# Fewer and larger loads of queries and keys in a two-layer attention kernel on Trainium2

## The chip, the cores and the metric

One core of a Trainium2 chip runs the whole program. The metric is device time in microseconds (us) of one execution. The core has five engines with a queue of instructions each: PE (matrix products), DVE (vector operations), ACT (activations), POOL (further elementwise work) and SP, which in this kernel does nothing but issue DMA transfers. An engine takes its instructions strictly in order. The DMA transfers themselves run on 16 DMA engines, here called lanes.

## The reference

A sequence `x` of 2048 rows of width 256 goes through two transformer layers with 16 heads of width 16. Cut to what matters:

```
layer 0, h = first or second half of the rows (1024 each):
  x_h += gate * attend(q(norm(x_h)), k(norm(x_h)), v(norm(x_h))) @ wo      # stage 0: own half
  x_h += gate * attend(q(norm(x_h)), k(norm(x_other)), v(norm(x_other)))   # stage 1: other half
  x_h += gate * mlp(norm(x_h))
layer 1, all 2048 rows:
  scores = where(mask == 0, -1e9, q @ k.T / 4)
  x = norm(x + softmax(scores) @ v @ wo)                                   # stage 2: masked
  x = norm(x + attend(q(x), k(ctx), v(ctx)) @ wo)                          # stage 3: 1601 context rows
  x = norm(x + mlp(x))
```

`attend` is a softmax over the keys. For it the kernel finds the maximum of every row of scores first, and computes the scores a second time, transposed, less that maximum.

## The kernel before

**Units.** The rows are cut into 4 blocks of 512 (`BLK`), the 16 heads into 4 groups `g` of 4 heads. A unit is one block and one group in one of the four stages; the first block of the masked stage is done in two parts, each over half the keys, which gives 68 units. Keys lie in two slots of 1024 (`SLOT`). A unit of stage 0 or 1 sees one slot, one of stages 2 and 3 both. `stream` (line 1411) walks the units. A unit has two steps for each 128 keys (16 steps for 1024 keys). In each step PE computes one tile of transposed scores of this unit, ACT takes its exponential, PE multiplies an earlier tile by the values, and PE and DVE make one or more tiles of the row maxima of the next unit (`take_maxima`). The maxima of a unit begin four steps before the unit ahead of it does (`AHEAD`), that is in step 12 of a 16-step unit for the unit after next.

**Order.** The order on every engine is written by hand. `after(step)` (1472) runs once a step: it runs what stands in the list `later` and is due, sends at most one transfer from the list `transfers` (`load_ready`, line 989), and advances one of the background generators, which do projections, norms, the MLPs and the next stage's queries, keys and values. What has no place of its own on SP is issued in the order in which the program comes to it. SP waits at the head of its queue for the data and the buffer of its next transfer, with all others behind it.

**Through DRAM.** `halves` (461) computes queries and keys for a block, splits each into a high and a low part (`hi`, `lo`, in buffers tagged `half`, three of them) and stores them to `q_dr` and `k_dr`. `load_queries` (1002) loads a unit's queries, each high and each low part into two places, with 8 transfers of 16 partitions, 64 KB each; it is called in step 1 of a unit for the unit after next, into one of three buffers `q`. `load_slot` (932) puts 8 transfers of keys (16 partitions, 128 KB each) and two or more of values for one group and one slot into `transfers`. Four such sets of keys come ready in a row when the last block behind a slot is done.

**Sums.** In step 2 of the next unit `copy_sums` (1285) lets ACT copy a unit's accumulated products to `sums` (a `half` buffer). Four transfers bring the softmax sums to `weights`, four more the products to `oT`. Five steps later DVE inverts `weights` (`invert`, 1327), `rd` goes to DRAM (`rd_dr`) and comes back spread over 64 partitions (`rd_rows`, line 1337, whose source has an outermost dimension of 4), eight steps later POOL multiplies (`divide`, 1340). After ten or eleven steps the block's projection may start. In the unit done in parts, `as_rows` (1177) also sends the maxima on with 12 small transfers (`mh`, line 1194) and adds them on DVE four steps later.

**Masks.** `mask_rows` (1025) loads a 128x512 piece of the mask into one of two buffers `raw`, and POOL turns it into a bias. `mask_part` (1049) puts eight of these one step apart; `pair` in `maxima` (1123) does the next block's 16 pieces in group 3, two at a time where the unit is a part.

Of the kernel before, what the change touches and what calls it, by code (L numbers as in the profile page):

```python
# [12 lines left out]
F32 = mybir.dt.float32  # L13
# [9 lines left out]
P = 128  # L23
# [54 lines left out]
def two_layers(ctx: ExitStack, tc: tile.TileContext, a: dict, out: bass.AP):  # L78
# [76 lines left out]

    made = sb.tile([P, P], F32, tag="half", bufs=3, name="made")
    make_identity(nc, made)
# [43 lines left out]
    def half(shape, dtype=F32, name="half"):  # L201
        return sb.tile(shape, dtype, tag="half", bufs=3, name=name)

# [24 lines left out]
    def load_attn(n, raw_tile, between=None):  # L228
        w = a[f"w_attn{n}"]
        t = sb.tile([P, 2, 2, 2, P], F32, tag="w_qk", name="w_qk")  # L230
        for k in range(2):
            raw = raw_tile()
            nc.sync.dma_start(raw, w[:, k * 2 * BLK : (k + 1) * 2 * BLK])
            src = raw.rearrange("p (w g c i r) -> p w c g i r", w=2, g=NG, c=2, i=2)


            def copies(k=k, src=src):
                for qk in range(2):
                    for c in range(2):
                        nc.gpsimd.tensor_copy(  # L240
                            t[:, k, qk, c, :].rearrange("p (g i d) -> p g i d", g=NG, i=2),
                            src[:, qk, c, :, :, :HD],
                        )

            if between is None:
                copies()
            else:
                first_copies.append(copies)
# [75 lines left out]
    for g in range(NG):  # L324
        for i in range(2):
            at = (2 * g + i) * HD
            for c in range(2):
                (nc.sync, nc.scalar)[i].dma_start(qkb[at : at + HD, :, :, c], src[g, i, c, :HD])
    m = one_ps()
# [418 lines left out]
    def chain_cross(b):  # L748
# [4 lines left out]
        if last:  # L753
# [4 lines left out]
        yield from normalize(xn, t, 1e-6)  # L758
        hT = yield from transposed(xn, mod=(2, b // 2))
        yield from mlp(  # L760
            mlp0[0], 0, AF.Gelu_apprx_tanh, hT, gated(rows["m0"], t, b),

            (lambda: mask_part(1)) if last else None,
        )
# [28 lines left out]
    def chain_context(n):  # L793

        if n == 0:

            yield 20
            load_attn(3, attn_raw)
        r0, r = CTX[n]
        c = stage([P, TPB, D], name="c")  # L800
# [4 lines left out]
        if r % P:  # L805
            nc.sync.dma_start(c[: r % P, full, :], a["ctx"][r0 + full * P : r0 + r, :])
        yield 3
        hT = yield from transposed(c, n=r)
# [123 lines left out]
    def load_slot(kind, st, g, slot):  # L932
# [7 lines left out]
        def keys(c, i):  # L940
            at = 64 * c + HD * i
            nc.sync.dma_start(
                kT[g][slot][at : at + HD, :, :even].bitcast(F32),
                d[c, i % 2, 2 * g * HD : (2 * g + 2) * HD, :even].rearrange(
                    "(q d) t -> d q t", d=HD
                ),
            )
# [23 lines left out]
        if kind == "keys":  # L971
            if st == 2 and slot == 1 and g in (1, 2):
                kT[g][slot] = sb.tile([P, 2, SLOT], F32R, tag=f"kT{g}{slot}", name="kT")
            transfers.extend(
                (what, lambda c=c, i=i: keys(c, i)) for c in range(2) for i in range(4)
            )
# [25 lines left out]
    def load_queries(u):  # L1002
        st, b, g = u["st"], u["b"], u["g"]
        ensure(("q", st, b))
        u["q"] = sb.tile([P, 2, BLK], F32R, tag="q", bufs=3, name="q")
        d = queries_dr[st, b]
        for c in range(2):
            for i in range(4):
                at = 64 * c + HD * i
                nc.sync.dma_start(  # L1010
                    u["q"][at : at + HD].bitcast(F32),
                    d[c, i // 2, 2 * g * HD : (2 * g + 2) * HD, :].rearrange(
                        "(q d) t -> d q t", d=HD
                    ),
                )
# [32 lines left out]

    def mask_part(slot):

        for n in range(2 * TPB):
            later.append([n, lambda n=n: mask_rows(SPLIT, slot, n // 2, n % 2), False])

# [20 lines left out]
    def maxima(u):  # L1074
# [48 lines left out]
        def pair(qt, n, i):  # L1123
            begin()
            if masked and i == 0 and g == NG - 1 and 1 in u["slots"]:
                at = ORDER[2].index(b) + 1
                each = 2 * 2 // len(chunks)
                for j in range(n * each, (n + 1) * each) if at < NB else ():
                    mask_rows(ORDER[2][at], j // 2, qt, j % 2)
            s = big_ps()  # L1130
# [46 lines left out]
    def as_rows(u):  # L1177
# [10 lines left out]
        if "part" in u:  # L1188

            t = sb.tile([P, NPART, 4 * BLK // P], BF16, tag="mh", bufs=2, name="mh")  # L1190
            for j in range(4):
                for h in range(NPART):
                    r = 64 * (j // 2) + 2 * h + j % 2
                    nc.sync.dma_start(  # L1194
                        t[PH * j : PH * (j + 1), h, :], u["nm"][r : r + 1, :]
                    )

# [5 lines left out]

            later.append([4, add, False])

# [79 lines left out]
    def copy_sums(u):  # L1285
# [15 lines left out]
        else:  # L1301
            u["weights"] = sb.tile([P, 4 * BLK // P], F32, tag="rd", bufs=4, name="weights")
        for j in range(4):
            nc.sync.dma_start(
                u["weights"][PH * j : PH * (j + 1), :], sums[PH * j + ONE : PH * j + ONE + 1, :]
            )
        at = (g % 2) * (P // 2)
# [103 lines left out]
    def stream(stages, start_up):  # L1411
# [91 lines left out]
        for u in units:  # L1503
# [4 lines left out]
            for s2 in range(len(second)):  # L1508
                if masked:
                    evict()  # L1510
                if s2 == 3:
                    pending += values_of(u)
                if s2 == 1 and i + 2 < len(units):
                    load_queries(units[i + 2])
# [169 lines left out]
```

## Time and profile before

| what | us |
|---|---|
| median of 3 runs (3054.51 to 3059.77) | 3057.54 |
| the profiled execution | 3064.13 |
| its span | 3062.4 |
| PE busy in the span | 2826.0 |
| DVE busy | 2174.5 |
| ACT busy | 1721.8 |
| POOL busy | 388.9 |
| 16 lanes, mean busy share: queue of SP | 24.7% |

The span is the time from the program's first to its last instruction in the profiled execution. Busy times are those of one engine; an engine's idle time counts only where the chain of waits runs through it. Issues on SP are marked SPq and are not counted as busy. In the chain of waits and the timeline a line begins with its start in us from the span's start and its length in us.

### The profile page before, as it was taken

The page shows a single profiled execution, that of the slowest core. Times are in us where ns is not written, and L with a number is a line of the kernel's source. Part 1 is how long each engine was busy: PE and PEld are TensorE (multiplying, and loading weights), DVE is VectorE, ACT ScalarE, POOL GpSimd, SP SyncE. Part 2 cuts the span into 40 slices and gives each one's busy share as a digit, 9 for nine tenths or more (in the row PEclk, how much of TensorE's full clock was granted, in tenths as well). Part 3 has the DMA queues.
Part 4 walks back from the last instruction along what each step waited for, and adds up shares of the span by engine and source line. Part 5 has one row for each costly group of instructions (what it writes and reads, how often), then busy time and mean ns, then how long its engine had stood idle before and what let it go on. Part 6 is the DMA issues. An engine that isn't in the chain of part 4 may idle for free.

```text
span 3062.4 us, 71795 instructions
## 1 busy us (share of the span) xinstructions
PE 2826.0 (92%) x30040; PEld 1258.6 (41%) x30040; DVE 2174.5 (71%) x3856; ACT 1721.8 (56%) x1897; POOL 388.9 (13%) x333
## 2 busy tenths in 40 slices
PE   6999999989998999786999999999999999999997
PEld 2334433333343344333444444444434444444442
DVE  5777777766766577465878878877768858858562
ACT  1466666665655556343555565565556746657472
POOL 0001101101010210203212101301001011110110
PEclk8999999999999999898999999999999999999998
DMA  7652262261205321443212001102242000100000
GB/s 220 143 97 92 67 109 66 75 115 34 73 28 110 60 78 42 108 92 104 68 31 65 29 21 53 55 19 60 46 68 84 24 21 27 28 21 23 21 22 12
DMA packets 178640, 192.11 MB, mean 63 GB/s; under 512 B 95476, under 2 KB 112380, under 8 KB 178316
## 3 DMA queue, kind: packets, MB, share of 16 engines
q1 hardware_dynamic: 177164, 187.52, 24.7%
q8 instruction: 236, 3.87, 0.6%
q14 instruction: 88, 0.72, 0.1%
q10 hardware_dynamic: 1152, 0.00, 0.0%
HBM read 129.78 MB, written 48.45 MB: 58 GB/s over the span
## 4 chain that ended last, share of the span: by engine, by line
PE 73%; DVE 9%; DMA 8%; SPq 4%; ACT 3%; issue 2%; POOL 1%; DVEq 0%; ACTq 0%; POOLq 0%
PE m_ps L1268 20%; PE m_ps L113 12%; PE s_ps L1241 11%; PE s_ps L1232 11%; PE s_ps L1142 8%; PE s_ps L1224 5%; DVE pm L1156 3%; DVE s_ps L1149 2%; PE s_ps L1136 2%; ACT e L1251 1%; DMA rd_dr<-rd 1%; DMA kT<-k_dr 1%; PE s_ps L113 1%; SPq L1194 1%; DVE t L413 1%
## 5 line engine op out<-in xcount | busy, mean ns | idle before, releaser
L1251 ACT ACTIVATE e<-s_ps 128x1024 f32<-128x1024 f32 (+1 forms) x1440 | 1474.0, 1024 | 1054.6 <-PE s_ps L1241 570.0
L1156 DVE TENSOR_REDUCE pm<-s_ps 128x2 f32<-128x1024 f32 x896 | 1090.6, 1224 | 315.2 <-PE s_ps L1142 300.3
L1268 PE MATMUL m_ps<-e,V 128*32 128x256 f32 (+1 forms) x11520 | 928.9, 393 | 11.8 <-DVE lo L496 11.6
L1149 DVE CUSTOM_DVE_ANT_0 s_ps<-s_ps,bias 128x512 f32<-128x512 f32 x1024 | 713.2, 700 | 211.2 <-PE s_ps L1136 191.0
L1241 PE MATMUL s_ps<-q,kT 64*128 64x512 f32 (+1 forms) x2880 | 805.5, 555 | 0.0
L1142 PE MATMUL s_ps<-kT,q 64*128 64x512 f32 (+2 forms) x2560 | 689.0, 436 | 45.9 <-DMA kT<-k_dr 19.3
L1232 PE MATMUL s_ps<-nm,sel 64*128 64x512 bf16 (+1 forms) x2880 | 567.9, 391 | 40.7 <-DVE pm L1156 28.9
L1268 PEld LDWEIGHTS m_ps<-e,V 128*32 128x32 f32 (+1 forms) x11520 | 250.2, 109 | 339.6 <-issue 236.1
L1142 PEld LDWEIGHTS s_ps<-kT,q 64*128 64x128 f32 x2560 | 295.9, 190 | 190.2 <-ACT e L1251 124.6
L1232 PEld LDWEIGHTS <-sel 64*128 64x128 bf16 (+1 forms) x2880 | 144.7, 93 | 506.2 <-issue 470.3
L1241 PEld LDWEIGHTS s_ps<-q,kT 64*128 64x128 f32 (+1 forms) x2880 | 281.6, 192 | 117.2 <-issue 117.2
L1136 PE MATMUL s_ps<-kT,q 64*128 64x256 f32 x1024 | 291.2, 366 | 3.5 <-DMA kT<-k_dr 2.7
L1344 POOL TENSOR_TENSOR oT<-oT,rd_rows 64x512 f32<-64x512 f32 x63 | 80.1, 1271 | 1592.3 <-DMA rd_rows<-rd_dr 1304.7
L1224 PE MATMUL s_ps<-biasT,ident 64*64 64x512 bf16 x2048 | 210.8, 402 | 9.8 <-DVE pm L1149 7.9
L1136 PEld LDWEIGHTS s_ps<-kT,q 64*128 64x128 f32 x1024 | 194.3, 193 | 18.2 <-DMA kT<-k_dr 3.2
L1044 POOL TENSOR_SCALAR bias<-raw 128x512 bf16<-128x512 int32 x64 | 123.0, 1922 | 274.6 <-DMA raw<-in_mask 258.2
L1224 PEld LDWEIGHTS <-ident 64*64 64x64 bf16 x2048 | 58.5, 103 | 223.7 <-issue 188.1
L1149 DVE DVE_READ_ACCUMULATOR2_ANT pm<- 128x1 f32 x1024 | 144.9, 142 | 0.0
L113 PE MATMUL m_ps<-hT,w_qk 128*32 128x512 f32 (+2 forms) x928 | 112.8, 604 | 12.8 <-DVE lo L496 10.2
L496 DVE SCALAR_TENSOR_TENSOR lo<-m_ps,qkb,hi 128x512 fp32r<-128x512 f32 (+3 forms) x62 | 43.5, 701 | 113.7 <-ACT hi L495 55.6
L113 PE MATMUL m_ps<-w_mlp,hid 128*32 128x256 f32 x1792 | 105.2, 388 | 11.2 <-ACT sums L1298 11.2
L113 PE MATMUL m_ps<-hT,w_mlp 128*32 128x512 f32 x896 | 107.7, 598 | 7.3 <-ACT sums L1298 4.3
(123 smaller groups left out, 1334.7 us busy)
## 6 DMA issues: line engine op xcount, KB each, us to landing
q<-q_dr SPq DMA_DIRECT2D x544, 64.0 KB
kT<-k_dr SPq DMA_DIRECT2D x192, 128.0 KB
raw<-in_mask SPq DMA_DIRECT2D x64, 256.0 KB
oT<-sums SPq DMA_DIRECT2D x256, 32.0 KB
rd_rows<-rd_dr SPq DMA_DIRECT2D x63, 128.0 KB
q_dr<-hi SPq DMA_DIRECT2D x30, 256.0 KB
q_dr<-lo SPq DMA_DIRECT2D x30, 256.0 KB
k_dr<-hi SPq DMA_DIRECT2D x24, 256.0 KB
```

The lines of the kernel that those rows point to most:

```text
L113: nc.tensor.matmul(m[at:to], lhsT=lhsT[:, at:to], rhs=rhs, start=start, stop=stop)
L1044: nc.gpsimd.tensor_scalar(bias_rows[b, slot, qt][:, j * BLK : (j + 1) * BLK], raw, 0.0, MASKED, ALU.is_equal, ALU.mult,)
L1136: nc.tensor.matmul(exchanged(s[:, h, :], part), lhsT=queries(qt, h, i), rhs=exchanged(keys(slot, c, x, h, i), 1 - part), start=True, stop= ...
L1142: nc.tensor.matmul(s[:, h, at : at + x], lhsT=queries(qt, h, i), rhs=keys(slot, c, x, h, i), start=True, stop=True,)
L1149: nc.vector.tensor_tensor_reduce(out=s[:, h, :], in0=s[:, h, :], in1=bias_rows[b, slot, qt][:, c : c + BLK], scale=1.0, scalar=-3.0e38, op ...
L1156: nc.vector.tensor_reduce(u["pm"][:, qt, :, i, n], s, AX.X, ALU.max)
L1224: nc.tensor.matmul(s[to : to + 64, h, :], lhsT=ident16[of : of + 64, of : of + 64], rhs=bias_columns[b, slot, kt][of : of + 64, :], start= ...
L1232: nc.tensor.matmul(s[:r, h, :], lhsT=sel[64 * h : 64 * h + 64, i, :r], rhs=u["nm"][64 * h : 64 * h + 64, :], start=not masked, stop=masked,)
L1241: nc.tensor.matmul(s[:r, h, :], lhsT=kT[g][slot][64 * h : 64 * h + 64, i, kt * P : kt * P + r], rhs=u["q"][64 * h : 64 * h + 64, i, :], st ...
L1251: nc.scalar.activation(e[:r], s[:r], AF.Exp, scale=SCALE)
L1268: nc.tensor.matmul(u["av"][PH * j : PH * (j + 1), cut], lhsT=V[g][slot][:r, kt * GW + j * VW : kt * GW + j * VW + PH], rhs=u["e"][n, j % 2 ...
L1344: nc.gpsimd.tensor_tensor(v, v, u["rd"], ALU.mult)
```

## The change

- Queries and keys are stored in another order of rows: the two heads that share a place (`q` in the code, 0 or 1) lie next to each other for each of the 16 elements `d`, so that one partition's two rows are one run in DRAM. For this POOL's copies of the weights (line 240) and the loads of the biases `qkb` (328) write with a stride of two.
- `load_queries` issues 4 transfers of 32 partitions, 128 KB each. The source is given a leading dimension of 2 with stride 0, which repeats the same 16 rows for the second place.
- `load_slot` issues 4 transfers of 32 partitions, 256 KB each, for slots of 1024 keys (stages 0 to 2); the source's leading dimension is 2, high and low part. Stage 3, with 896 and 706 keys, keeps its 8.
- The query load moves from step 1 of a unit to step 3, behind the transfers of `copy_sums` in step 2.
- `weights` comes in one transfer instead of four. `mh` comes in 6 instead of 12, one a step and from two steps later on, and is added 12 steps later instead of 4.
- Mask pieces: every two steps instead of every step; half of slot 1's before the last MLP of stage 1 instead of after it; the next block's 16 one at a time over groups 2 and 3 of the second part.
- `half` gets a fourth buffer. The load of stage 3's weights starts 4 instead of 20 steps into the context chain.

```diff
--- before.py
+++ after.py
@@ -153,7 +153,7 @@
             entry[1].pop(0)()
 
 
-    made = sb.tile([P, P], F32, tag="half", bufs=3, name="made")
+    made = sb.tile([P, P], F32, tag="half", bufs=4, name="made")
     make_identity(nc, made)
     identR = sb.tile([P, P], F32R, tag="identR", name="identR")
     nc.vector.tensor_copy(identR, made)
@@ -199,7 +199,7 @@
         return sb.tile(shape, dtype, tag="stage", bufs=2, name=name)
 
     def half(shape, dtype=F32, name="half"):
-        return sb.tile(shape, dtype, tag="half", bufs=3, name=name)
+        return sb.tile(shape, dtype, tag="half", bufs=4, name=name)
 
     def hidden(shape, dtype=F32, name="hid"):
         return sb.tile(shape, dtype, tag="hidden", bufs=HB, name=name)
@@ -238,7 +238,7 @@
                 for qk in range(2):
                     for c in range(2):
                         nc.gpsimd.tensor_copy(
-                            t[:, k, qk, c, :].rearrange("p (g i d) -> p g i d", g=NG, i=2),
+                            t[:, k, qk, c, :].rearrange("p (g d i) -> p g i d", g=NG, i=2),
                             src[:, qk, c, :, :, :HD],
                         )
 
@@ -323,9 +323,11 @@
     nc.scalar.activation(sc2, c2, AF.Silu)
     for g in range(NG):
         for i in range(2):
-            at = (2 * g + i) * HD
+            at = 2 * g * HD
             for c in range(2):
-                (nc.sync, nc.scalar)[i].dma_start(qkb[at : at + HD, :, :, c], src[g, i, c, :HD])
+                (nc.sync, nc.scalar)[i].dma_start(
+                    qkb[at + i : at + 2 * HD : 2, :, :, c], src[g, i, c, :HD]
+                )
     m = one_ps()
     for k in range(2):
         nc.tensor.transpose(m[:, 2 * k : 2 * k + 2], sc2[:, k * P : (k + 1) * P], ident[:2, :2])
@@ -757,10 +759,12 @@
         xn = stage([P, TPB, D], name="xn")
         yield from normalize(xn, t, 1e-6)
         hT = yield from transposed(xn, mod=(2, b // 2))
+        if last:
+            mask_part(1, 0, TPB)
         yield from mlp(
             mlp0[0], 0, AF.Gelu_apprx_tanh, hT, gated(rows["m0"], t, b),
 
-            (lambda: mask_part(1)) if last else None,
+            (lambda: mask_part(1, TPB, TPB)) if last else None,
         )
         if last:
             rows["a3"] = load_rows(10, 3)
@@ -794,8 +798,9 @@
 
         if n == 0:
 
-            yield 20
+            yield 4
             load_attn(3, attn_raw)
+            yield 16
         r0, r = CTX[n]
         c = stage([P, TPB, D], name="c")
         full = r // P
@@ -804,7 +809,7 @@
         )
         if r % P:
             nc.sync.dma_start(c[: r % P, full, :], a["ctx"][r0 + full * P : r0 + r, :])
-        yield 3
+        yield 4
         hT = yield from transposed(c, n=r)
         yield from keys_and_values(3, hT, n, r)
 
@@ -939,11 +944,16 @@
 
         def keys(c, i):
             at = 64 * c + HD * i
+            mine = slice(2 * g * HD, (2 * g + 2) * HD)
+            if even == SLOT:
+                nc.sync.dma_start(
+                    kT[g][slot][at : at + 2 * HD].rearrange("p q t -> p (q t)").bitcast(F32),
+                    d[c, :, mine, :].rearrange("i (d q) t -> i d (q t)", d=HD),
+                )
+                return
             nc.sync.dma_start(
                 kT[g][slot][at : at + HD, :, :even].bitcast(F32),
-                d[c, i % 2, 2 * g * HD : (2 * g + 2) * HD, :even].rearrange(
-                    "(q d) t -> d q t", d=HD
-                ),
+                d[c, i % 2, mine, :even].rearrange("(d q) t -> d q t", d=HD),
             )
 
         def values(j, n):
@@ -972,7 +982,8 @@
             if st == 2 and slot == 1 and g in (1, 2):
                 kT[g][slot] = sb.tile([P, 2, SLOT], F32R, tag=f"kT{g}{slot}", name="kT")
             transfers.extend(
-                (what, lambda c=c, i=i: keys(c, i)) for c in range(2) for i in range(4)
+                (what, lambda c=c, i=i: keys(c, i))
+                for c in range(2) for i in range(0, 4, 2 if even == SLOT else 1)
             )
         else:
             transfers.extend(
@@ -1005,13 +1016,12 @@
         u["q"] = sb.tile([P, 2, BLK], F32R, tag="q", bufs=3, name="q")
         d = queries_dr[st, b]
         for c in range(2):
-            for i in range(4):
-                at = 64 * c + HD * i
+            for i in range(2):
+                at = 64 * c + 2 * HD * i
+                src = d[c, i, 2 * g * HD : (2 * g + 2) * HD, :].rearrange("(d q) t -> d (q t)", d=HD)
                 nc.sync.dma_start(
-                    u["q"][at : at + HD].bitcast(F32),
-                    d[c, i // 2, 2 * g * HD : (2 * g + 2) * HD, :].rearrange(
-                        "(q d) t -> d q t", d=HD
-                    ),
+                    u["q"][at : at + 2 * HD].rearrange("p q t -> p (q t)").bitcast(F32),
+                    src.unsqueeze(0).to_broadcast([2, HD, 2 * BLK]),
                 )
 
 
@@ -1046,10 +1056,12 @@
             ALU.is_equal, ALU.mult,
         )
 
-    def mask_part(slot):
-
-        for n in range(2 * TPB):
-            later.append([n, lambda n=n: mask_rows(SPLIT, slot, n // 2, n % 2), False])
+    def mask_part(slot, first=0, n_rows=2 * TPB):
+
+        for n in range(first, first + n_rows):
+            later.append(
+                [2 * (n - first), lambda n=n: mask_rows(SPLIT, slot, n // 2, n % 2), False]
+            )
 
     def mask_columns(b, slot, kt):
 
@@ -1122,11 +1134,11 @@
 
         def pair(qt, n, i):
             begin()
-            if masked and i == 0 and g == NG - 1 and 1 in u["slots"]:
+            if masked and i == 0 and 1 in u["slots"]:
                 at = ORDER[2].index(b) + 1
-                each = 2 * 2 // len(chunks)
-                for j in range(n * each, (n + 1) * each) if at < NB else ():
-                    mask_rows(ORDER[2][at], j // 2, qt, j % 2)
+                k = (g - NG) * TPB * len(chunks) + qt * len(chunks) + n + 4 * TPB
+                if k >= 0 and at < NB:
+                    mask_rows(ORDER[2][at], k % 4 // 2, k // 4, k % 2)
             s = big_ps()
             at = 0
             for slot, c, x in chunks[n]:
@@ -1188,12 +1200,12 @@
         if "part" in u:
 
             t = sb.tile([P, NPART, 4 * BLK // P], BF16, tag="mh", bufs=2, name="mh")
-            for j in range(4):
-                for h in range(NPART):
-                    r = 64 * (j // 2) + 2 * h + j % 2
-                    nc.sync.dma_start(
-                        t[PH * j : PH * (j + 1), h, :], u["nm"][r : r + 1, :]
-                    )
+            def fetch(j, h):
+                r = 64 * j + 2 * h
+                nc.sync.dma_start(t[64 * j : 64 * (j + 1), h, :], u["nm"][r : r + 2, :])
+
+            for n in range(2 * NPART):
+                later.append([2 + n, lambda n=n: fetch(n // NPART, n % NPART), False])
 
             def add():
                 n = u["minus"] = part_tile(u, "minus")
@@ -1201,7 +1213,7 @@
                 for h in range(2, NPART):
                     nc.vector.tensor_tensor(n, n, t[:, h, :], ALU.add)
 
-            later.append([4, add, False])
+            later.append([2 * NPART + 6, add, False])
 
     def part_tile(u, name):
         return sb.tile([P, 4 * BLK // P], F32, tag=f"{name}{u['g']}{u['part']}", name=name)
@@ -1300,10 +1312,7 @@
             u["weights"] = part_tile(u, "weights")
         else:
             u["weights"] = sb.tile([P, 4 * BLK // P], F32, tag="rd", bufs=4, name="weights")
-        for j in range(4):
-            nc.sync.dma_start(
-                u["weights"][PH * j : PH * (j + 1), :], sums[PH * j + ONE : PH * j + ONE + 1, :]
-            )
+        nc.sync.dma_start(u["weights"], sums[ONE:P:PH, :])
         at = (g % 2) * (P // 2)
         if first_part:
             dst = first_sums[g] = dr.tile([P // 2, BLK], F32, tag="o", bufs=NG, name="o_dr")
@@ -1510,7 +1519,7 @@
                     evict()
                 if s2 == 3:
                     pending += values_of(u)
-                if s2 == 1 and i + 2 < len(units):
+                if s2 == 3 and i + 2 < len(units):
                     load_queries(units[i + 2])
 
                 if masked:
```

## The prediction

> **What bounds the kernel now.** I read the page first. Its busy line and its chain line:
>
> ```profile
> PE 2826.0 (92%) x30040; PEld 1258.6 (41%) x30040; DVE 2174.5 (71%) x3856; ACT 1721.8 (56%) x1897; POOL 388.9 (13%) x333
> ...
> PE 73%; DVE 9%; DMA 8%; SPq 4%; ACT 3%; issue 2%; POOL 1%; DVEq 0%; ACTq 0%; POOLq 0%
> ```
>
> PE is busy 2826.0 of 3062.4 us, so 236 us is all that better transfers could ever give. DMA and SP's issuing hold 12% of the chain. The chain in order of time shows where; this is the start of the masked stage:
>
> ```profile
> 1258.11 0.48 ACT nm L1187
> 1258.61 0.51 SPq L1194
> ...
> 1265.49 0.59 SPq L1194
> 1266.12 0.58 SPq L942
> ...
> 1269.08 5.62 DMA kT<-k_dr
> ...
> 1274.78 0.76 PE s_ps L1136 x2
> ```
>
> PE waits for keys that stand on SP behind the twelve `mh` issues of 0.59 us. The same row of twelve stands on the chain at 1361.5 and at 1416.6. Next, SP's timeline of an ordinary unit of stage 0, and the start-up on PE:
>
> ```profile
> 319.59 3.81 SPq L1010 DMA_DIRECT2D q<-q_dr  x8
> 325.43 2.44 SPq L1304 DMA_DIRECT2D weights<-sums  x4
> 327.91 2.50 SPq L1313 DMA_DIRECT2D oT<-sums  x4
> 332.53 0.34 SPq L1335 DMA_DIRECT2D rd_dr<-rd  x1
> 335.13 0.58 SPq L1337 DMA_DIRECT2D rd_rows<-rd_dr  x1
> ```
> ```profile
> 41.69 0.76 PE L1142 MATMUL s_ps<-kT,q 64*128 64x512 f32 x1 [7.66 <-DMA kT<-k_dr]
> ```
>
> The queries issued at 319.59 have all landed at 325.2 (the last step of their completion counts in the trace); counting the 32 maxima products of each unit of stages 0 and 1, their first use is at 336.27: 11.1 us to spare. Over the units of stages 0 and 1 this spare time is 3 to 37 us, in stages 2 and 3 mostly 25 us and more.
>
> **How wide a transfer is.** This decides the case. In the trace a transfer's completion count climbs once per lane that served it. A key load of 16 partitions climbs 16 times. `rd_rows`, whose source has an outermost dimension of 4, jumps at 1.0 us after its issue and then climbs 4 times, at 3.22 to 3.59 us (the one at 2341.3). Loads and stores whose outermost dimension is 2 (`ada_b`, `mod_dr`) climb twice. So a transfer is served by as many lanes as its outermost dimension allows, and the new query and key loads, outermost dimension 2 in the source, will run on 2 lanes instead of 16. A narrow transfer also holds up what comes behind: `first` at 1549.29, issued 0.67 us after a load that used 4 lanes, landed 12 of its 16 parts by 2.91 us and the other 4 at 4.28 to 4.85 us.
>
> One lane's rate is in the trace's packet records: on each of `rd_rows`' four lanes 2 KB packets follow every 80 ns, 4 KB packets take 159 ns and 8 KB ones 307 ns when little else runs. That gives:
> - Queries of a unit, now: 8 x 2 packets per lane x 84 ns = 1.3 us. After: 4 transfers x 16 packets of 4 KB x 159 ns = 10.2 us on two lanes.
> - A set of keys, now: 8 x 2 x 159 ns = 2.5 us. After: 4 x 16 packets of 8 KB x 312 ns = 20 us on two lanes.
>
> No row shows whether every narrow transfer takes the same two lanes. From below: if they take turns, several run beside each other and nothing is late (rival 1). From above: the same two, and they queue. I take the second, since the operands carry counts of elements and nothing that would choose a lane. [...] No run here shows which.
>
> Every wide transfer leaves a sixteenth of itself on these two lanes, and so lands no sooner than they are free. The moved query load adds no wait: SP stands there for ACT's `sums` in any case. But SP keeps only 8 transfers in flight (its semaphores 100 to 108 go round, and nearly every issue waits for its own), so a backlog holds SP too.
>
> **The sum, part by part.**
>
> *Stretches where four or eight sets are loaded.* Work on the two lanes is sets x 20 + units' queries x 10.2 + a sixteenth of all other bytes. The latter come from the stretch's GB/s times its length, less keys (0.13 MB an issue) and queries (0.066 MB), at 25.6 GB/s a lane:
>
> ```profile
> 30.00:173.00 143.00, 117.70 (x1049) 45.95 (x1042) 98.66 (x129) 57.50 (x63) 5.60 (x13) 0.89 0.67 155
> 375.00:425.00 50.00, 47.00 (x504) 19.44 (x496) 38.29 (x38) 32.94 (x35) 1.28 (x1) 1.00 0.59 114
> 607.00:662.00 55.00, 49.77 (x494) 20.53 (x492) 37.82 (x38) 32.90 (x35) 3.27 (x9) 0.94 0.60 123
> ```
>
> Start-up: 155 GB/s x 143 us = 22.2 MB, less 56 key and 40 query issues, leaves 12.2 MB, 30 us a lane. One transfer leaves the list per step, and with 4 instead of 8 for a set all eight sets are ahead of unit 4's queries. From the first query issue at 30.6: 8 x 20 + 5 x 10.2 + 30 = 241, so these land at 272 instead of before 172.9, where unit 4's maxima began: +99. In the same way, to the first use of the queries that stand last behind the keys: from 375.5, 80 + 20 + 6 = 106, use at 425.4: +56. From 606.9, 80 + 20 + 7, use at 661.7: +52. From 928.5, 80 + 20 + 8, use at 985.4: +52. From 1257.2, 80 + 20 + 13, use at 1354.3: +16. Together 275. This lets the lanes be busy without a break; I add 30 for breaks (some 5% of the 675 us of work), with 0 and 135 (20%) as bounds.
>
> What is late there: the queries, and `weights`, for which DVE waits in its order (L1330 waited 49.7 us in 9 places already); behind it stand the maxima that free PE's score tiles.
>
> *Ordinary units of stages 0 and 1.* `copy_sums` issues at 325.43 as before; one `weights` (0.59) and four `oT` (2.5) later, at 328.5, come the queries; 1.2 to the first packet, 10.2, 0.2 to the count: 340.1 instead of 325.2, 14.9 later. Spare time is under 14.9 outside the stretches in units 6, 8, 9, 10, 16, 17, 18, 25, 26, 33 and 34 (11.6, 9.7, 11.6, 11.1, 9.8, 10.4, 11.4, 13.7, 11.3, 13.9, 10.8): together +39 (bounds 0, if lanes take turns, and 60). In stages 2 and 3 the longer units hide it.
>
> *The way from sums to projection.* `rd_dr` at 332.53 now stands behind the queries until 340 and `rd_rows` lands 5 us later. PE waits for POOL's product already at 460.9, 699, 997, 2294.6 and 2458 to 2837, so it is not covered there: 7 x 5 = +35 (bounds 0 and 60).
>
> *Gains.* Six `mh` fewer, the rest one a step: off the chain three times 7.5 = 22. The mask pieces no longer stand four at a time on SP ahead of key stores (9.70 us at 1241.06, 8.19 at 1408.38), the fourth `half` takes away DVE's waits for a free one (19.6, 13.8 and 12.3 us, most beside PE's work): some 20 more. 201 `weights` and 368 query and key issues fewer at 0.4 to 0.6 us would take most of L1330's waits, which I call 10. In all 52 where the loads are not narrow; 30 where they are, since most of it lies in stretches that the lanes now set. Bounds 0 and 60. POOL's copies with stride two: 32 of 303 ns, 9.7 us, beside waits for `w_raw`; twice as long would cost under 10 us, nothing on the chain. At nothing I put `qkb` (16 issues as before), the context chain (its 16 steps change places with a load that POOL awaits), the sum over `mh` (8 steps later, read only a unit or more after that) and `weights` itself (128 packets of 64 B on 4 lanes, at some 11 ns 0.35 us); were the last two awaited, it would be their few us in eight units.
>
> 3064.1 + 275 + 30 + 39 + 35 - 30 = 3413. The runs' median is 6.6 us below the profiled execution, so 3407; I say **3405**.
>
> **Rivals.**
> 1. *Not slower: the lanes take turns, or the loads are wide after all.* A set then costs about its old time, and the gains remain: 3057.5 - 52 = 3005. For it: with `mh` 617 issues fewer, and `mh` on the chain. Against: the counts of `rd_rows`, `ada_b` and `mod_dr`. Decides if four query loads land within 5 us of their issue.
> 2. *Slower by little: narrow, but keys are wanted so far ahead that only queries are late.* Stage 1's first keys land by 450 us and are first used at 519. It needs the sums not to stand behind the keys: 3057.5 + 39 + 35 + 20 (the first set, for which PE waits at 41.69) - 30 = 3122. Against: the 12 + 4 landings of `first`.
> 3. *Slower by more: SP, held by its 8 transfers in flight, lets the lanes fall idle between queries and sums; breaks of 30% or more,* 200 instead of 30: 3575. For it: SP already waits with other work behind it (L1010, 409 us for PE). Against: keys are popped a step apart and keep the lanes fed.
>
> **How the numbers follow.** Forecast 0.78, rival 1 0.09, rival 2 0.08, rival 3 0.05. The terms' own bounds reach from 3405 - 30 - 39 - 35 - 30, that is 3270, to 3405 + 105 + 21 + 25 + 30 = 3586; not all go one way. Reaching a little towards rival 2, the range is 3200 to 3540. A measurement of this kernel tells 0.2% (6 us) from no change. Faster 0.09, same 0.01, slower 0.90.
>
> **What would show it.** Query and key loads whose counts climb twice; query landing 11 to 12 us after issue; waits of PE's maxima (L1142) for `q` and `kT` of 100 us and more, and of L1330 for `weights` above 49.7; PE's slices thin at 0 to 300, around 400, 650, 950 and 1300 us, and as full as before from 1455 to 2270; PE's busy time unchanged. I am wrong if the counts climb 16 times, or if narrow loads issued together land together.

## The result, and the profile after

| | before | after |
|---|---|---|
| median us (4 runs each, side by side) | 3058.65 (3054.51 to 3067.92) | 3548.08 (3538.7 to 3550.67) |
| span of the profiled execution | 3062.4 | 3546.1 |
| PE busy | 2826.0 | 2911.3 |
| PE idle (span less busy) | 236 | 635 |
| time at half the granted clock (sum of the clock records at 0.5) | 182 | 691 |

The changed kernel takes 1.157 [1.1549, 1.1591] of the time before. The predicted 3405 us lies 143 us below, and the range's upper end 8 us below.

From the page of the kernel before, PE's busy tenths in 40 slices of 77 us and the granted clock in the same slices, in tenths of full speed:

```profile
PE   6999999989998999786999999999999999999997
...
PEclk8999999999999999898999999999999999999998
```

The page of the kernel after: its span, busy times, PE's busy tenths in 40 slices of 89 us, the granted clock in the same slices, and the shares of the chain of waits.

```profile
span 3546.1 us, 70882 instructions
...
PE 2911.3 (82%) x30040; PEld 1282.7 (36%) x30040; DVE 2182.2 (62%) x3856; ACT 1722.9 (49%) x1897; POOL 390.0 (11%) x333
...
PE   5566886588378884998757999999998999989897
...
PEclk7787998799689986999878999999999999999998
...
PE 59%; DMA 22%; SPq 8%; DVE 7%; issue 2%; ACT 2%; POOL 1%; ACTq 0%; POOLq 0%; DVEq 0%
```

DMA and SP's issuing went from 12% to 30% of the chain. DVE, ACT and POOL do the same work in the same time (2182.2 against 2174.5 us for DVE). PE does the same 30040 products, idles 398 us more and is *busy* 85 us more. The slices are thin up to some 1950 us (stages 0 and 1 and the start of the masked stage) and nearly full from there.

The waits of PE before and one of DVE, then the same after (engine, line and tile, what it waited for: us in all, times, longest). L1154 is the maxima product that had line 1142 before, L1339 the inversion of the sums (1330 before), L1244 the first product into a fresh score tile (1232 before).

```profile
PE s_ps L1232 <- DVE pm L1156: 28.9, 41, 3.2
PE m_ps L113 <- POOL oT L1344: 19.8, 7, 6.6
...
DVE rd L1330 <- DMA weights<-sums: 49.7, 9, 14.6
```

```profile
PE s_ps L1244 <- DVE pm L1168: 204.6, 45, 42.1
PE s_ps L1154 <- DMA q<-q_dr: 125.5, 32, 8.5
...
PE m_ps L113 <- POOL oT L1353: 40.4, 4, 15.5
PE s_ps L1154 <- DMA kT<-k_dr: 39.3, 4, 20.2
```
```profile
DVE rd L1339 <- DMA weights<-sums: 213.4, 8, 46.6
```

Two kinds of waits are new or far longer. Thirty-two short ones for queries, 3.9 us each, are spread over the units. And eight long ones of DVE for `weights`, 27 us each in the mean, (before nine of at most 14.6) are there; seven fall in the stretches where keys are loaded, and the eighth, 11.6 us until 3460, near the end of the run. DVE stands in its order before the maxima, so the maxima come late, the score tiles stay taken, and PE waits at L1244 for DVE. That line of PE names DVE, but the cause is DVE's own wait for a transfer: the longest, 46.6 us of DVE until 1387.3, is followed by one of 42.1 us of PE that ends at 1388.7.

**Two lanes.** SP's timeline of the kernel after in an ordinary unit (start, length, line, transfer):

```profile
479.64 2.64 SPq L1022 DMA_DIRECT2D q<-q_dr  x4
483.54 0.32 SPq L1344 DMA_DIRECT2D rd_dr<-rd  x1
```

The completion count of each of the four query loads climbs only twice. They are issued 0.6 us apart, but land at 484.6, 487.2, 489.7 and 492.3: one every 2.55 us. That is one queue of 4 x 2.55 = 10.2 us, as if nothing but two lanes existed. `rd_dr` behind them, a store whose count climbs 16 times, has 14 of its 16 parts done 1.24 to 2.56 us after its issue, and the last two at 8.89 and 8.92 us, that is 0.15 us after the two parts of the last query load. Fourteen parts went ahead at once and two stood behind the queries. The view of the lanes shows the same: tenths of 16 lanes busy and GB/s, in 40 slices of 0.5 us from 478 to 498 us.

```profile
DMA  2112201011113111111111111110000035999300
GB/s 49 41 41 66 62 4 16 16 57 49 57 49 94 51 50 66 49 49 49 49 66 49 49 49 49 57 57 18 0 0 0 16 125 176 342 211 307 123 10 0
```

From 482 to 491.5 us the core moves some 50 GB/s with a tenth of its lanes; the wide load at the end reaches 342.

**What SP and the sums pay.** From the chain of waits of the kernel after, in the stretch where the second four sets of keys are loaded (start, length, what):

```profile
575.57 24.63 DMA rd_dr<-rd
...
605.33 16.30 SPq L949
...
622.99 22.95 DMA kT<-k_dr
...
646.60 10.02 DMA q<-q_dr
...
656.75 0.76 PE s_ps L1154
```

An 8 KB store takes 24.63 us because two of its sixteen parts stand behind keys: 14 land by 577.97, the last two at 599.55 and 600.20, 0.6 us after the two parts of the last key load ahead of them (598.96 and 599.65). From 577.97 to 599.55 the 16 lanes are busy 0.13 of the time in the mean. One key issue on SP, otherwise 0.6 us, takes 16.30, until 621.63. It does not wait for its semaphore, one of the eight that SP's transfers use in turn in this trace: the transfer that had it before landed at 604.01, and only six were under way when it began. Four of them were narrow key loads; what limit the issue ran into is not settled. Then PE's next maxima have to wait for keys and for queries, one after the other.

**PE slower for the same products.** Three answers by stretches of time, one of the kernel before and two of the kernel after (from:to, length, busy time and number of instructions of PE, PE's weight loads, DVE, ACT, POOL, then granted clock, share of the lanes, GB/s). The first two hold the same 233 products of one unit; the third shows shorter stretches around two waits:

```profile
313.00:336.30 23.30, 23.30 (x233) 9.43 (x231) 20.50 (x21) 17.45 (x19) 1.28 (x1) 1.00 0.13 35
```
```profile
456.00:488.00 32.00, 26.60 (x233) 10.22 (x229) 21.18 (x23) 18.09 (x20) 1.27 (x1) 0.89 0.09 28
```
```profile
456.00:461.00 5.00, 0.85 (x5) 0.18 (x1) 1.03 (x4) 1.37 (x2) 0.00 (x0) 1.00 0.13 49
461.00:468.00 7.00, 5.95 (x33) 2.35 (x33) 2.79 (x3) 1.72 (x2) 1.27 (x1) 0.51 0.06 20
...
485.00:492.00 7.00, 2.80 (x27) 0.94 (x19) 2.92 (x5) 2.78 (x3) 0.00 (x0) 0.99 0.13 51
492.00:498.50 6.50, 6.08 (x37) 2.38 (x39) 2.92 (x3) 1.86 (x2) 1.27 (x1) 0.50 0.35 101
498.50:505.00 6.50, 6.50 (x101) 3.35 (x100) 3.90 (x4) 2.72 (x4) 2.20 (x2) 0.99 0.01 3
```

The unit's products take 26.60 us busy instead of 23.30. The short stretches show why. In this unit PE waits 5.16 us for queries until 462.1, the clock is granted at 0.50 from 461.1 to 467.9, and 33 products take 5.95 us. The last three lines show the next wait as a whole: 4.62 us until 492.4, the clock at 0.50 for 6.8 us from 491.8, in which 37 products take 6.08 us, then back at 0.99, where 101 products take 6.50. The kernel after has 26 waits of PE of 4 to 6 us (from 30 us on), and after every one the clock is at 0.50 for another 3.7 us or more. These waits are paid twice, once as idle time and once, afterwards, as slow products.

### The profile page after: what moved, and what is told of

Its sections match the earlier page's. It is cut to its first block, busy times and chain, and to the rows that moved or that the text cites. A ratio compares the mean times of both kernels' runs of the same rounds, so it can differ in the third digit from the quotient of the medians.

```text
span 3546.1 us, 70882 instructions
## 1 busy us (share of the span) xinstructions
PE 2911.3 (82%) x30040; PEld 1282.7 (36%) x30040; DVE 2182.2 (62%) x3856; ACT 1722.9 (49%) x1897; POOL 390.0 (11%) x333
## 4 chain that ended last, share of the span: by engine, by line
PE 59%; DMA 22%; SPq 8%; DVE 7%; issue 2%; ACT 2%; POOL 1%; ACTq 0%; POOLq 0%; DVEq 0%
PE m_ps L1280 16%; PE m_ps L113 10%; PE s_ps L1253 9%; PE s_ps L1244 8%; DMA q<-q_dr 7%; PE s_ps L1154 6%; DMA kT<-k_dr 5%; PE s_ps L1236 4%; DMA rd_dr<-rd 4%; SPq L949 3%; DVE pm L1168 2%; DMA v_dr<-v 2%; PE s_ps L1148 1%; SPq L1022 1%; DMA q_dr<-hi 1%
## 5 line engine op out<-in xcount | busy, mean ns | idle before, releaser
L1280 PE MATMUL m_ps<-e,V 128*32 128x256 f32 (+1 forms) x11520 | 950.0, 401 | 2.6 <-DVE lo L498 2.4
L1154 PE MATMUL s_ps<-kT,q 64*128 64x512 f32 (+2 forms) x2560 | 710.8, 445 | 209.2 <-DMA q<-q_dr 125.5
L1253 PE MATMUL s_ps<-q,kT 64*128 64x512 f32 (+1 forms) x2880 | 823.8, 568 | 0.0
L1244 PE MATMUL s_ps<-nm,sel 64*128 64x512 bf16 (+1 forms) x2880 | 578.0, 398 | 211.8 <-DVE pm L1168 204.6
L1154 PEld LDWEIGHTS s_ps<-kT,q 64*128 64x128 f32 x2560 | 304.2, 195 | 362.5 <-issue 198.2
L1244 PEld LDWEIGHTS <-sel 64*128 64x128 bf16 (+1 forms) x2880 | 144.7, 93 | 695.1 <-issue 660.4
L1148 PEld LDWEIGHTS s_ps<-kT,q 64*128 64x128 f32 x1024 | 196.5, 195 | 59.9 <-issue 40.9
L1339 DVE RECIPROCAL rd<-weights 128x16 f32<-128x16 f32 x59 | 14.5, 246 | 213.4 <-DMA weights<-sums 213.4
L497 ACT ACTIVATE hi<-m_ps,qkb 128x512 fp32r<-128x512 f32 (+3 forms) x62 | 40.2, 648 | 176.9 <-PE m_ps L113 100.3
```

The source lines that it names most:

```text
L1148: nc.tensor.matmul(exchanged(s[:, h, :], part), lhsT=queries(qt, h, i), rhs=exchanged(keys(slot, c, x, h, i), 1 - part), start=True, stop= ...
L1154: nc.tensor.matmul(s[:, h, at : at + x], lhsT=queries(qt, h, i), rhs=keys(slot, c, x, h, i), start=True, stop=True,)
L1244: nc.tensor.matmul(s[:r, h, :], lhsT=sel[64 * h : 64 * h + 64, i, :r], rhs=u["nm"][64 * h : 64 * h + 64, :], start=not masked, stop=masked,)
L1253: nc.tensor.matmul(s[:r, h, :], lhsT=kT[g][slot][64 * h : 64 * h + 64, i, kt * P : kt * P + r], rhs=u["q"][64 * h : 64 * h + 64, i, :], st ...
L1280: nc.tensor.matmul(u["av"][PH * j : PH * (j + 1), cut], lhsT=V[g][slot][:r, kt * GW + j * VW : kt * GW + j * VW + PH], rhs=u["e"][n, j % 2 ...
```

## The experiments

Ratios are to the kernel before, run beside each kernel, with 95% intervals.

**wide8: queries and keys wide, all else of the change kept.** Eight transfers of 16 partitions as before, on the new order of rows.

```diff
-                    kT[g][slot][at : at + 2 * HD].rearrange("p q t -> p (q t)").bitcast(F32),
-                    d[c, :, mine, :].rearrange("i (d q) t -> i d (q t)", d=HD),
+                    kT[g][slot][at : at + HD].rearrange("p q t -> p (q t)").bitcast(F32),
+                    d[c, i % 2, mine, :].rearrange("(d q) t -> d (q t)", d=HD),
...
-                    src.unsqueeze(0).to_broadcast([2, HD, 2 * BLK]),
+                    src.rearrange("(d q) t -> d (q t)", d=HD),
```

> The changed kernel with queries and keys of stages 0 to 2 loaded by 8 transfers of 16 partitions again (new order of rows kept, 4 KB and 8 KB runs), so that every source's outermost dimension is 16. Theory (two lanes, always the same, serve a narrow load, and all else queues behind them): the whole loss goes, counts climb 16 times, 3000 to 3030 us, some 30 to 50 under the kernel before. Rival (the loss comes from the later query load, or from the new order of rows): stays above 3300.

Measured: 3019.97 us, 0.9846 [0.9823, 0.987]. The whole loss is gone with the width, and what is left of the change gains 45 us. PE is busy 2832.6 us, about as before (2826.0).

**q_wide and k_wide: only the queries, only the keys wide** (each with its half of the edit above).

> The changed kernel with the queries alone wide again, keys narrow. Theory: the stretches with key sets stay slow, ordinary units and stage 3 recover; two lanes' work in the stretches without queries gives 55 + 39 + 35 + 35 = 164 us late, a quarter more for PE's lower clock after waits, 30 of gains: 3200 to 3260. Rival (keys are wanted far ahead, only queries are late): 3010 to 3040.

> The changed kernel with the keys alone wide again, queries narrow. Theory: every unit of stages 0 and 1 loses 5 to 10 us (wait for the second half of the queries, then PE at half clock for some us), stage 3 some 9 a block, the stretches go: 3190 to 3270. Rival (only queries are late): about as slow as the changed kernel, 3500.

Measured: q_wide (keys narrow) 3298.48 us, 1.0753 [1.0728, 1.0779], which is 38 us above what was expected; k_wide (queries narrow) 3266.24 us, 1.0647 [1.0618, 1.0675]. Above wide8, narrow keys cost 0.0907 and narrow queries 0.0801, together 0.1708; both at once cost 1.157 - 0.9846 = 0.1724. The two add up, so they hardly hide each other. Their waits differ. First q_wide, waits of PE and of DVE, then k_wide, waits of PE:

```profile
PE s_ps L1244 <- DVE pm L1168: 214.6, 45, 44.2
...
DVE rd L1339 <- DMA weights<-sums: 224.8, 8, 48.2
```
```profile
PE s_ps L1154 <- DMA q<-q_dr: 107.5, 28, 8.8
...
PE s_ps L1244 <- DVE pm L1168: 20.4, 35, 2.1
```

Narrow keys alone give all of the long waits behind `weights`; narrow queries alone give the short ones, and of the waits for `weights` only 13.5 us in all are left. PE's busy time tells the clock's part: 2842.8 us in q_wide (few long waits, 10 above wide8) and 2889.0 in k_wide (many short ones, 56 above). The 10 and 56 make most of the 79 of the changed kernel (2911.3 less 2832.6).

**wide4: four transfers as in the change, but wide.** The sixteen elements `d` become the outermost dimension, the two parts or the repetition the next.

```diff
-                    d[c, :, mine, :].rearrange("i (d q) t -> i d (q t)", d=HD),
+                    d[c, :, mine, :].rearrange("i (d q) t -> d i (q t)", d=HD),
...
-                    src.unsqueeze(0).to_broadcast([2, HD, 2 * BLK]),
+                    src.unsqueeze(1).to_broadcast([HD, 2, 2 * BLK]),
```

(The eight key transfers of a stage 3 set take the same partition order, 32 partitions each.)

> The changed kernel with as few transfers as it has (4 of 32 partitions for queries, 4 for a set of keys), but with the 16 elements as the source's outermost dimension and the two copies or parts inside it, so that partitions alternate between them; stage 3's keys in 8 transfers of 32 partitions. Theory: counts climb 16 times with 32 partitions in one transfer; as fast as the 8 transfers or a few us faster, 2990 to 3025. Rival (a transfer of 32 partitions or of fewer, larger runs is itself slow): above 3300.

Measured: 2970.7 us, 0.9684 [0.9661, 0.9707], 19 us below the expected interval. The same number of transfers of the same size as in the changed kernel, only with another dimension outermost, takes some 577 us less. Here are wide4's lanes around a query load issued at 315.17, again in slices of 0.5 us, from 313.5 to 333.5:

```profile
DMA  2122208494502000000026999410000010000000
GB/s 45 37 49 66 57 8 254 131 270 172 197 25 44 4 0 1 0 0 0 4 74 158 320 268 295 156 37 0 0 0 0 0 33 0 0 0 0 0 0 0
```

What took 9.5 us at 50 GB/s with a tenth of the lanes busy is over in 2.5 us at 131 to 270 with four to nine tenths. And four transfers instead of eight, with the other partition order of stage 3's keys, are worth 49 us (wide8 to wide4), once both are wide.

**narrow_s1 and wide4_s1: the query load back in step 1,** with narrow loads and with wide ones.

```diff
-                if s2 == 3 and i + 2 < len(units):
+                if s2 == 1 and i + 2 < len(units):
```

> The changed kernel, narrow loads and all, with the query load back in step 1, ahead of the sums. Theory: in ordinary units of stages 0 and 1 the narrow queries then land some 6 to 9 us earlier, before their use, and PE keeps its clock; the stretches with keys stay: 3440 to 3490, of the 490 lost some 60 to 110 come back. Rival (the later place costs nothing): 3535 to 3560. Other rival (sums behind narrow queries cost as much as the queries saved): the same or above.

> The kernel with 4 wide transfers, query load back in step 1. Theory of the prediction (sums behind 4 query transfers delay weights, on which DVE stands): 8 to 20 us slower than with the load in step 3, 2979 to 2991. Rival (wide queries take so little of the lanes that their place is nothing): within 4 us, 2967 to 2975.

Measured: narrow_s1 3422.04 us, 1.1145 [1.113, 1.1161]; wide4_s1 2960.18, 0.9639 [0.9626, 0.9652], and once more on another chip (wide4_s1b) 2965.96, 0.9665 [0.9645, 0.9685], a little above the 0.963 to 0.965 expected.

> The fastest kernel so far once more (4 wide transfers, query load in step 1), beside the three that take something from it: 0.963 to 0.965 of the kernel before.

With narrow loads the move costs 126 us, more than I had expected: before the sums, the queries do not stand behind `oT`, and each ordinary unit gets some 7 to 8 us back (by the first maxima product of each unit). DVE's waits for `weights` become longer instead, since they now stand behind the queries (narrow_s1, waits of DVE):

```profile
DVE rd L1339 <- DMA weights<-sums: 300.3, 28, 56.1
```

With wide loads I expected the new place to gain 8 to 20 us; by the medians it loses 5 to 10 (by the ratios 0.0019 to 0.0045, 6 to 14 us). The interval of wide4_s1 lies just below that of wide4, that of wide4_s1b overlaps it. The reason is not settled. wide4 still has 5.9 us of waits for queries on PE and wide4_s1 has none, which fits; DVE's waits for `weights` go the other way, 17.9 us in wide4 and 25.8 in wide4_s1.

**Single parts taken back out of wide4 or wide4_s1.** wide4_mh12 puts the twelve `mh` transfers back, all at once, added four steps later; wide4_half3 has three `half` buffers; s1_w4 loads `weights` in four; s1_mask has the masks and the context chain as before.

```diff
...
-            for n in range(2 * NPART):
-                later.append([2 + n, lambda n=n: fetch(n // NPART, n % NPART), False])
+            for j in range(4):
+                for h in range(NPART):
+                    r = 64 * (j // 2) + 2 * h + j % 2
+                    nc.sync.dma_start(t[PH * j : PH * (j + 1), h, :], u["nm"][r : r + 1, :])
...
-    made = sb.tile([P, P], F32, tag="half", bufs=4, name="made")
+    made = sb.tile([P, P], F32, tag="half", bufs=3, name="made")
...
-        nc.sync.dma_start(u["weights"], sums[ONE:P:PH, :])
+        for j in range(4):
+            nc.sync.dma_start(
+                u["weights"][PH * j : PH * (j + 1), :], sums[PH * j + ONE : PH * j + ONE + 1, :]
+            )
...
-            mask_part(1, 0, TPB)
...
-            (lambda: mask_part(1, TPB, TPB)) if last else None,
+            (lambda: mask_part(1)) if last else None,
...
-                [2 * (n - first), lambda n=n: mask_rows(SPLIT, slot, n // 2, n % 2), False]
+                [n - first, lambda n=n: mask_rows(SPLIT, slot, n // 2, n % 2), False]
```

> The kernel with 4 wide transfers, with the twelve mh transfers at once again and the sum over them 4 steps later. Theory of the prediction (7.5 us three times on the chain of waits): 15 to 25 us slower, 2986 to 2996. Rival (other waits take their place): under 6 us.

> The kernel with 4 wide transfers and three half buffers again. Theory of the prediction (DVE's waits of 19.6, 13.8 and 12.3 us for a free buffer, mostly beside PE's work): 3 to 12 us slower, 2974 to 2983. Rival (ACT and DVE hold PE up through them in full): 20 to 45 us slower.

> The same with weights in four transfers again. Theory (SP's 0.6 us an issue stands ahead of DVE's inverse only where SP is behind): 0 to 12 us slower. Rival (each unit's chain of sums is on PE's way): 1.8 us for each of 30 units of stages 0 and 1 and 4 of stage 3, 40 to 60 us slower.

> The same with the mask pieces and the context chain in the places of the kernel before. Theory of the prediction (9.7 and 8.2 us of SP standing on raw, partly hidden): 8 to 18 us slower, all between 1230 and 1500 us of the span. Rival (nothing): within 4 us.

| kernel | us | ratio | beside | worth of the part |
|---|---|---|---|---|
| wide4_mh12 | 2982.42 | 0.9721 [0.9706, 0.9737] | wide4 0.9684 | 11 us |
| wide4_half3 | 2973.94 | 0.9687 [0.9672, 0.9702] | wide4 0.9684 | nothing |
| s1_w4 | 2974.26 | 0.969 [0.967, 0.971] | wide4_s1b 0.9665 | 8 us |
| s1_mask | 2972.54 | 0.9685 [0.9664, 0.9706] | wide4_s1b 0.9665 | 7 us |

Of these only the first stands clear when both intervals are counted, barely; the 7 and 8 us are at the edge of what can be told. The fourth `half` buffer is worth nothing that can be measured, which fits waits for a free one that lay beside other work.

**before_wide4: the kernel before with the new order of rows and four wide transfers alone.**

> The kernel before with nothing changed but the order of rows and the 4 wide transfers for queries and for keys. Theory (fewer issues and fewer steps until a set of keys is loaded are the larger part of the gain): 35 to 65 us faster than the kernel before, 0.979 to 0.989. Rival (issues of queries and keys were hidden; mh, masks and weights make the gain): within 12 us of the kernel before.

Measured: 3019.57 us, 0.9841 [0.982, 0.9862], a gain of 51 us. The parts add up to 51 + 11 + 8 + 7 = 77 of the 105 us that wide4_s1b gains; the rest belongs to none alone and was not settled. wide4_s1 is the fastest version found, 3.4 to 3.6% below the kernel before. Its page, busy times and slices of PE:

```profile
PE 2807.3 (95%) x30040; PEld 1250.3 (42%) x30040; DVE 2177.7 (74%) x3856; ACT 1721.0 (58%) x1897; POOL 389.2 (13%) x333
...
PE   7899999999999999999999999999999999999996
```

Its PE is busy 19 us less than in the kernel before, and the time at half clock is 101 us against 182: fewer waits, faster products.

## Why the prediction was right in kind and too small

The best view of the sum is the shift of each unit: the start of its first maxima product, after less before, worked out from the two traces.

| part of the run | shift gained there, us | predicted |
|---|---|---|
| start-up, to unit 4 | 113 | 99 |
| the four later stretches with keys (72, 68, 61, 28) | 229 | 176 (56, 52, 52, 16), and 30 for breaks in all five |
| between them, units of stages 0 and 1 and the first of stage 2 (45, 28, 19, 4) | 96 | 39, and part of the 35 below |
| stages 2 and 3 (units 38 to 67) | 46 | the rest of the 35 |
| all | 484 | 349 with 30 of gains taken off |

**Width: right.** "A transfer is served by as many lanes as its outermost dimension allows" fits what the kernel after shows: the counts of the new loads, with 2 outermost, climb twice, those of a `rd_rows` with 4 (issued at 600.22) four times and those of an `oT` with 16 (563.77) 16 times. wide8 (3019.97 us) and wide4 (2970.7) take the whole loss away by nothing but another outermost dimension.

**The same two lanes, a queue: right.** The prediction could not show it. Here it is seen in the cadence of 2.55 us and in the 14 + 2 parts of `rd_dr`. From 484.6 to 492.3 the four loads land one behind the other, as on the same two lanes; which two of the sixteen, no trace here tells. Lanes in turn (rival 1, 3005) fell. So did rival 2 (3122, keys not late): with the keys alone narrow the kernel is still 1.0753.

**Rates: right.** 10.2 us for a unit's queries was worked out and is what they took.

**"PE's busy time unchanged": wrong.** This is the step that failed. Of the 484 us, 398 are idle time of PE and 85 are busy time, and the sum of 349 held idle time only. So of the missing 135 us 85 are products that took longer, and the other 50 are waits. Most of the 85 is the clock: inside the spells at 0.50 PE is busy 289 us, against 113 before (129 in wide8, 148 in q_wide, 244 in k_wide). A batch of eight products takes 1.08 us there instead of 0.64, so the 175 us more hold some 71 us of stretching, an estimate from these numbers; the other 14 are not settled. By runs, k_wide has 56 us more than wide8 and 31 waits for queries, 1.8 us each. The granted clock stood in the page before, 8 to 9 tenths in every slice, and in each row by stretches; I read it as a given and did not ask what new waits do to it.

**Ordinary units: too small, 39 against some 96.** The term took "landing 14.9 later, less spare time" for eleven units. It left out the slow products after each wait. It also took each unit's spare time from the undisturbed kernel, where the loads ahead were not late yet; how much that makes was not measured.

**Stretches: 305 with breaks against 342.** The lane's work was sized well. Rival 3 (3575, SP held by its transfers in flight) came closest to the time, and SP is held: 16.30 us at one key issue, though not by the count of eight. But its breaks of 30% are not there. Laid end to end before their landings (2.55 us for a query load, 4.98 for a key load, as they land one behind the other), the narrow loads leave 13 of the 116 us from 541.0 to 656.6 free, 19 of the 121 from 872.2 to 993.1 and 46 of the 254 from 34.7 to 288.4. That is 11 to 18%, and the other transfers' sixteenths take a part of it (in the start-up 30 us by the prediction's sum). It is an estimate from the landings. How much of the 37 is SP's and how much the clock's stays open.

**From sums to projection: 35 against 46** in stages 2 and 3 alone, four block ends of stage 3 at 9.0 to 9.5 us instead of 5. In narrow_s1, where the queries go ahead of the sums, the same four shift by -0.5 to 2.6 us. The waits of PE for POOL's product went from 19.8 to 40.4 us.

**Gains: the sizes were wrong both ways.** The 30 taken off can't be seen in any stretch. Without narrow loads I said 52: 45 with eight wide transfers (wide8), but 95 with the four of the change made wide (wide4). The `mh` were put at 22 and are worth 11; masks and the fourth `half` at 20 and are worth 7 and nothing; `weights` and the query and key issues at 10, but `weights` alone is worth 8 and half the query and key transfers 49 to 51. What lay on SP in front of everything else was undervalued; what lay beside PE's work was overvalued.

**The moved query load "adds no wait": wrong in effect.** Its own issues wait for nothing new, but going back to step 1 saves 126 us with narrow loads, and perhaps 5 to 10 with wide ones.

## What to carry to other kernels

Before merging transfers, look at the outermost dimension of the source: with 2 there, half as many transfers made this kernel 1.157 of its time, and with 16 there (parts and repetitions one place further in) 0.968. The narrow loads were not only slow themselves here (one query load every 2.55 us), they held the last two of 16 parts of a store behind them (by 6.3 us until 492.4, by 21.6 us until 599.6), so look for the late ones among small stores and loads that were never touched. And when a change adds waits of a few us to PE, add the slow products after each to its price (here 1.08 us for a batch of eight instead of 0.64).

## What the hardware showed that was not expected

- After waits of 5.16 us (to 462.1) and 4.62 us (to 492.4) PE's clock was granted at 0.50 for 6.8 us each time, and a batch of eight products that takes 0.64 us took 1.08. The clock records here show 0.5 or 1.0 alone, and 43 of the 57 spells at 0.5 of the kernel after last 3.4, 6.8 or 10.2 us.
- Short waits came ahead of spells at 0.5 too. The one that begins at 263.1 us of the kernel after followed waits of PE of 0.32 and 1.17 us, the last until 262.1. Of the 77 spells that begin later than 90 us in the runs before and after, the one with the least idle time ahead of it had 1.49 us of it in the 3.4 us before it began. In the two cases above the clock was at 0.50 already in the last 0.95 and 0.6 us of the wait. PE's busy times are those of the profile, so these idle times are estimates.
- Loads whose counts climb only twice were enough to stop the core. An 8 KB store whose count climbs 16 times took 24.63 us, with the 16 lanes busy 0.13 of the time in the mean while its last two parts were out; 14 of 16 parts of another were there 6 us before its end; and one issue on SP took 16.30 us instead of 0.6, in which PE was busy for 0.10 us.
